# The opening of a scan kernel rearranged: x before the weights, weight products among the statistics, the second step's x and the first stores of silu asked for earlier

## The chip, the cores and the metric

The kernel runs on one core of a Trainium2 chip. The core has a matrix engine (TensorE, PE in the profile; its weight loads are listed apart, as PEld), a vector engine (VectorE, DVE), a scalar engine that applies functions and copies (ScalarE, ACT), a general engine (GpSimd, POOL) and an engine that here only issues transfers (SyncE, SP). Each engine works through its own instructions in the order in which they are written down; semaphores make one wait for another. Transfers between the chip's memory (DRAM) and the core run on 16 DMA engines, whoever issues them. Matrix products land in PSUM, which has eight banks.

The metric is the device time of one execution in microseconds (us), as a median of several.

## The reference

The input x is 4 images of 128 channels by 96 by 96 pixels, all in 32-bit floats. It is normalised in groups of four channels, goes through the block below, and is added to the result. Cut to what matters:

```python
def _scan1d(x, ...):                       # x: sequences of 9216 steps, 128 channels
    t = _grouped1x1(x, in_proj_w, in_proj_b, G)            # 128 -> 512, in 4 groups
    u, gate = (t[:, :HID], t[:, HID:])                     # HID = 256
    u = jax.nn.silu(u)
    u = depthwise_conv(u, dw_w)                            # 5 taps along the sequence
    s = _conv1x1(u, ssm_in_w)                              # 256 -> 32
    a = DMIN + (DMAX - DMIN) * jax.nn.sigmoid(_conv1x1(u, ssm_delta_w, ssm_delta_b))
    bb = jnp.tanh(_conv1x1(u, ssm_b_w, ssm_b_b))
    cc = jnp.tanh(_conv1x1(u, ssm_c_w, ssm_c_b))
    hst = recurrence(a, bb * s)                            # h[n] = a[n] * h[n-1] + bb[n] * s[n]
    u = u + _conv1x1(cc * hst + ssm_d[None, :, None] * s, ssm_out_w)
    u = _grouped1x1(u * jax.nn.sigmoid(gate), mix_w, mix_b, G)
    return _conv1x1(u, out_proj_w, out_proj_b)

seq_h = rows of the image one after the other;  seq_v = columns one after the other
y1, y2, y3, y4 = _scan1d(seq_h), _scan1d(seq_h reversed), _scan1d(seq_v), _scan1d(seq_v reversed)
x + fuse_w @ concat(y1, y2, y3, y4 put back in place) + fuse_b
```

The reference writes the recurrence with cumulative sums of logarithms. Three linear maps follow one another at the end (mix, output projection, fuse), so they can be multiplied into one matrix per direction beforehand.

## The kernel before

**Steps and units.** Two directions of the same image (forward and reversed) run together as s = 0 and s = 1. An image is scanned by columns, then by rows, in six steps each; a step has four positions p, and a unit is one step, position and direction, with 384 sequence elements in 128 by 384 tiles. Two units (s = 0, 1) make a pair; `pair(t)` on line 793 does the work of pair t, of which there are 192, and lets the later stages of a unit run six pairs (`LAG`) behind the first ones. The whole order is written out by hand (`tc.manual_schedule`): each engine gets its instructions in the order of the Python code.

**Stages of a pair.** `front` applies the input projection and silu to a quarter g of the following step (`in_proj`, line 486, products on PE from `x_in`; `silu`, line 493, on ScalarE into the tile `sil`, half of the channels for j = 0 and half for j = 1). `conv` and `conv_less` (613, 622) are the depthwise convolution of the j = 0 channels as products on PE. The j = 1 channels get it by `taps` (639): the first tap on ScalarE (line 649), the other four on VectorE (line 651), one after the other through the two PSUM banks TAPS, so that a pair's first tap cannot start before the last tap of the pair before. `proj` (663) takes u to the four small maps on PE; its evacuations (lines 683 to 689, tiles `tm` and `t`) are on ScalarE. `scan` (707) is the recurrence on VectorE. From pair 6 on come the gates, the output map, and `accumulate` (738), which applies the folded matrix `w_fin` and adds into `acc`.

**Transfers of x.** `x_in[s]` holds the step's x. `after_front` (460) asks for the next step's x as soon as a quarter's products have read the old one: rows of j = 1 for the quarter g, and after the last quarter the rows of j = 0 for all four quarters. The input projection of a quarter needs the j = 0 rows of all quarters and the j = 1 rows of its own. `keep_silu` (473) stores finished quarters of `sil` to DRAM, 770 KB each, because the second half of the steps reads the first half's silu again, mirrored. `load_chunks` (405) and `stats_chunks` (410) load the next image in chunks `xs` and take its statistics with `bn_stats` on VectorE. All these transfers are issued by SP, one after the other; the issue of a transfer waits until its target is free.

**The opening.** Before the first input projection the kernel needs the mean and variance of the first image. `load_x` (278) loads x in eight transfers into `acc`, and VectorE takes `bn_stats` of 24 chunks of 384 columns (line 282). In between, `load` (273) asks on ScalarE's queue for the three weight arrays: `small` (biases and taps), `fuse` (output, fuse and mix matrices) and `main` (input projection and small maps). PE multiplies the final matrices together as soon as `fuse` is there: eight products into `w_of` (line 364, evacuated on line 367), eight into `w_fin` (lines 371, 374), and twelve products with a single column for the bias `b_fin` (line 379). `stay_busy` (284) adds products whose result nobody reads. `stats_finish` (176) is a generator: it yields after each part, so that its caller puts other work between. Its parts: the aggregate of the statistics (line 184), a product with `gmean` that averages over the group (187), the same for the variance (199), the square root on ScalarE (207), the load of the silu table (209), the scaling of the input weights into `wn` (226), and products for the biases `bnorm` (235 and line 134). Then `start` (1001) runs the first step's projections in bursts and its silus, and the first pair's taps.

A 32-bit product shows as two matmul rows in the profile, one for each of its passes through the array. Line 134 is a helper, `mm`, through which most products go; tile names tell them apart.

Of the kernel before, what the change touches and what calls it, by code (L numbers as in the profile page):

```python
# [47 lines left out]
P = 128  # L48
# [8 lines left out]
R = 4  # L57
# [10 lines left out]
def conv_preact_kernel(  # L68
# [9 lines left out]
    nc = tc.nc  # L78
# [96 lines left out]

    def stats_finish(b):

# [94 lines left out]

    def load(src, name, pool=wp):
        t = pool.tile(list(src.shape), F32, tag=name, name=name)
        nc.scalar.dma_start(t, src)
        return t

    def load_x(chunks):
        for c, n in chunks:
            nc.sync.dma_start(accf[:, bass.ds(c * SC, n * SC)], xr[b0, :, bass.ds(c * SC, n * SC)])  # L280
            for e in range(c, c + n):
                nc.vector.bn_stats(stats_of(b0)[:, e, :], accf[:, bass.ts(e, SC)])

    def stay_busy(n):
        if n:
            nc.tensor.matmul(  # L286
                bank(free[0] ^ 1)[:, :n], w_fin[:, 0, 0, :],
                w_fin.rearrange("p d j c -> p (d j c)")[:, :n], start=True, stop=True,
                skip_group_check=True,
            )  # L290

# [32 lines left out]
    nc.vector.tensor_scalar_mul(  # L324
        w_proj[:, :, 2 * MH : 3 * MH], w_proj[:, :, 2 * MH : 3 * MH], 0.5
    )


# [17 lines left out]
    for s in range(2):  # L346
        for p in range(R):
            for k in range(2):
# [9 lines left out]
                )  # L358

    w_of = pp.tile([P, 4, 2, P], F32, name="w_of")  # L360
    for d in range(4):
        for j in range(2):
            pt = bank(2 * (d % 4) + j)
            nc.tensor.matmul(  # L364
                pt[:, :P], w_out[:, bass.ts(j, P)], w_fuse[:, d, :], start=True, stop=True
            )
            nc.scalar.copy(w_of[:, d, j, :], pt[:, :P])
    for d in range(4):
        for j in range(2):
            pt = bank(2 * (d % 4) + j)  # L370
            nc.tensor.matmul(
                pt[:, :P], w_mix[:, j, :], w_of[:, d, j, :], start=True, stop=True
            )
            nc.scalar.mul(w_fin[:, d, j, :], pt[:, :P], 0.5)
    pb = bank(0)
    terms = [(w_of[:, d, j, :], b_mix[:, j : j + 1]) for d in range(4) for j in range(2)]
    terms += [(w_fuse[:, d, :], b_out) for d in range(4)]
    for i, (lhsT, rhs) in enumerate(terms):
        nc.tensor.matmul(
            pb[:, 0:1], lhsT, rhs, start=(i == 0), stop=(i == len(terms) - 1)  # L380
        )
    nc.scalar.activation(b_fin, pb[:, 0:1], AF.Identity, bias=b_fuse)
    for _ in range(4):
        stay_busy(512)
    prep.__exit__(None, None, None)
# [45 lines left out]

    def front_parts(i, banks):
# [12 lines left out]
        if fresh(step):  # L445
            yield from compute_front(step, g, banks)
# [54 lines left out]

    def compute_front(step, g, banks):
# [160 lines left out]
    def proj(i, banks, apart=False):  # L663
# [129 lines left out]
    def pair(t):  # L793
# [104 lines left out]
        if t >= NU // 2 - 4:  # L898
            load_last(t)

        keep_silu((1, 2, 1, 0)[t] if t < R else 0)

# [131 lines left out]
    with tc.manual_schedule(  # L1034
        engines={
            nc.tensor.engine, nc.vector.engine, nc.scalar.engine, nc.gpsimd.engine, nc.sync.engine
        }
    ):
        start()
        for t in range(NU // 2):  # L1040
            pair(t)
        tail()
# [79 lines left out]
```

## Time and profile before

| | us |
|---|---|
| median of 4 runs | 1839.06 (1837.08 to 1843.52) |
| the profiled execution, time | 1835.29 |
| the profiled execution, span | 1833.5 |
| PE busy | 1806.9 (99% of the span) |
| ScalarE, VectorE, GpSimd busy | 1566.9, 1450.4, 1424.4 |

The profile is of one execution. Its page gives the busy time of each engine. The "windows" view gives the same for stretches of the span, with the clock that TensorE was granted (1.00 is full speed), the busy share of the DMA engines and the rate at which they moved data. The "chain of waits" is followed back from the last instruction: at each step to what released it. The "timeline" lists instructions in order of time, with like ones merged. Times in these views are in us from the span's start.

### The profile page before, as it was taken

The numbers are of one execution on the slowest core, as the hardware profiler recorded it, in microseconds if no ns is written. First come the engines' busy times: TensorE is split into PE (matmuls) and PEld (weight loads), VectorE is DVE, ScalarE is ACT, GpSimd is POOL, SyncE is SP. The second block draws the span as 40 slices with busy tenths as digits, with TensorE's granted clock in tenths as the row PEclk, the third lists the DMA queues.
The fourth block names the chain that finished last, engine by engine and source line by source line (L and its number), as shares of the span: only waits on it lengthen the run. The fifth ranks groups of instructions, "written<-read, shape, count | busy, mean of one in ns | idle before, by whom it ended". The sixth has DMA issues, their size and how long they took to land.

```text
span 1833.5 us, 57282 instructions
## 1 busy us (share of the span) xinstructions
PE 1806.9 (99%) x24068; PEld 653.9 (36%) x24068; DVE 1450.4 (79%) x1451; ACT 1566.9 (85%) x2762; POOL 1424.4 (78%) x1469
## 2 busy tenths in 40 slices
PE   7999999999999999999999999999999999999998
PEld 4233333333333333333333333333333333333333
DVE  5788878877878888877778888877877778777886
ACT  5888888988888888888898888888888888888974
POOL 2487887778777888787877888787877788887785
PEclk9999999999999999999999999999999999999999
DMA  6755563444975566244696547443576634635434
GB/s 206 186 193 180 159 191 113 161 143 142 301 233 181 168 182 199 101 143 140 209 299 208 165 162 211 136 154 110 162 233 226 231 127 152 192 105 178 148 122 156
DMA packets 147825, 321.18 MB, mean 175 GB/s; under 512 B 14192, under 2 KB 115696, under 8 KB 147568
## 3 DMA queue, kind: packets, MB, share of 16 engines
q1 hardware_dynamic: 147136, 316.56, 54.1%
q8 instruction: 190, 3.11, 0.7%
q10 hardware_dynamic: 432, 0.96, 0.1%
q14 instruction: 67, 0.55, 0.1%
HBM read 185.21 MB, written 132.25 MB: 173 GB/s over the span
## 4 chain that ended last, share of the span: by engine, by line
PE 95%; ACT 2%; DMA 1%; DVE 1%; issue 0%; SPq 0%; POOL 0%; ACTq 0%; DVEq 0%; POOLq 0%
PE psum L134 81%; PE psum L520 8%; PE psum L514 5%; DMA x_in<-in_xs 1%; ACT sil L495 0%; PE psum L286 0%; DMA fuse<-in_fuse 0%; DVE u L600 0%; ACT t L701 0%; PE psum L364 0%; ACT psum L649 0%; ACT t L689 0%; DMA out<-acc 0%; ACT u L632 0%; DVE psum L651 0%
## 5 line engine op out<-in xcount | busy, mean ns | idle before, releaser
L651 DVE SCALAR_TENSOR_TENSOR psum<-sil,small,psum 128x768 f32<-128x768 f32 x576 | 588.9, 1022 | 34.2 <-ACT psum L649 8.5
L134 PE MATMUL psum<-u,w_fin 128*32 128x384 f32 x6176 | 552.4, 487 | 0.2 <-ACT t L689 0.2
L600 DVE SCALAR_TENSOR_TENSOR u<-gate,psum 128x768 f32<-128x768 f32 x376 | 349.7, 952 | 253.9 <-ACT gate L537 117.7
L134 PE MATMUL psum<-u,main 128*32 128x384 f32 x6144 | 536.3, 490 | 0.1
L770 POOL TENSOR_TENSOR acc<-ys,acc 128x384 f32<-128x384 f32 x374 | 410.8, 1119 | 34.0 <-ACT ys L751 10.0
L724 POOL TENSOR_TENSOR t<-t,t 64x384 f32<-64x384 f32 x191 | 236.3, 1237 | 156.7 <-PE psum L514 79.3
L134 PEld LDWEIGHTS psum<-u,w_fin 128*32 128x32 f32 x6176 | 189.1, 110 | 321.5 <-issue 220.9
L134 PEld LDWEIGHTS psum<-u,main 128*32 128x32 f32 x6144 | 181.6, 110 | 327.9 <-issue 201.5
L691 POOL TENSOR_SCALAR t<-tm 64x384 f32<-64x384 f32 x191 | 177.1, 927 | 153.2 <-ACT tm L683 105.0
L528 ACT COPY psum<-u 128x768 f32<-128x768 f32 x352 | 276.7, 799 | 21.6 <-DVE u L651 10.2
L134 PE MATMUL psum<-sil,band 128*32 128x384 f32 x3072 | 286.1, 488 | 3.1 <-ACT ys L753 3.1
L725 POOL TENSOR_TENSOR t<-t,t 64x384 f32<-64x384 f32 x191 | 246.7, 1292 | 15.0
L520 PE MATMUL psum<-t,main 32*128 32x384 f32 x1536 | 242.1, 515 | 3.3 <-ACT psum L528 2.6
L649 ACT ACTIVATE psum<-sil,small 128x768 f32<-128x768 f32 x192 | 174.1, 907 | 63.9 <-DVE u L600 54.1
L537 ACT ACTIVATE gate<-psum,bnorm 128x384 f32<-128x384 f32 x384 | 192.8, 582 | 28.8 <-PE psum L514 26.8
L692 POOL TENSOR_TENSOR t<-t,tm 64x384 f32<-64x384 f32 x192 | 195.1, 1016 | 15.3
L651 DVE SCALAR_TENSOR_TENSOR u<-sil,small,psum 128x768 f32<-128x768 f32 x192 | 194.9, 1015 | 7.8
L495 ACT ACTIVATE sil<-psum,bnorm 128x385 f32<-128x385 f32 x384 | 192.1, 584 | 4.6 <-PE psum L134 2.4
L134 PE MATMUL psum<-sil,less 64*32 64x384 f32 x3072 | 168.2, 495 | 0.0
L514 PE MATMUL psum<-x_in,wn 32*128 32x384 f32 x768 | 162.0, 528 | 2.4 <-ACT u L632 1.3
L753 ACT COPY ys<-psum 128x384 f32<-128x384 f32 x281 | 130.1, 477 | 30.1 <-PE psum L134 27.1
L134 PEld LDWEIGHTS psum<-sil,band 128*32 128x32 f32 x3072 | 89.8, 109 | 174.7 <-issue 93.3
(92 smaller groups left out, 1503.0 us busy)
## 6 DMA issues: line engine op xcount, KB each, us to landing
sil<-sil SPq DMA_DIRECT2D x128, 770.0 KB, 6.9
kept<-gate SPq DMA_DIRECT2D x80, 768.0 KB, 3.8
gate<-kept SPq DMA_DIRECT2D x76, 768.0 KB, 5.2
x_in<-in_xs SPq DMA_DIRECT2D x192, 96.2 KB, 2.5
out<-acc SPq DMA_DIRECT2D x48, 384.0 KB, 8.2
acc<-in_xr SPq DMA_DIRECT2D x38, 384.0 KB, 7.2
xs<-in_xr SPq DMA_DIRECT2D x72, 192.0 KB, 4.9
x_in<-in_xs SPq DMA_DIRECT2D x184, 48.1 KB, 4.0
```

The costliest lines, as they stand in the source:

```text
L134: nc.tensor.matmul(o[r, : rhs.shape[-1]], lhsT, rhs, start=start, stop=stop, skip_group_check=True)
L495: nc.scalar.activation(sils[step][:, s, j, g, :], bank(bk)[:, : N + 1], AF.Silu, bias=bn[:, 1:2] if j else bn[:, 4 + g : 5 + g],)
L514: nc.tensor.matmul(bank(to)[:, :N], stats[un["b"]][0][r, s, :], x_in[s][r, q, off : off + N], start=True, stop=True)
L520: nc.tensor.matmul(bank(SSM + 2 * s + j)[:, :N], w_so[r, bass.ts(j, P)], z[r, :], start=bi not in seeded, stop=True, skip_group_check=True)
L528: nc.scalar.copy(psum[:, SSM + 2 * s : SSM + 2 * s + 2, :N], us[bi][:, s])
L537: nc.scalar.activation(gv[:, s, j, :], bank(to[2 * s + j])[:, :N], AF.Tanh, bias=bn[:, 2 + j : 3 + j], scale=0.5,)
L600: nc.vector.scalar_tensor_tensor(v, g, 1.0, pz, ALU.add, ALU.mult)
L651: nc.vector.scalar_tensor_tensor(us[i][:, :, 1, :] if k == K - 1 else part, src, w_tap[:, k : k + 1], part, ALU.mult, ALU.add,)
L692: nc.gpsimd.tensor_mul(ta[0:64, p, :], tb[0:64, :], tm[0:64, :])
L724: engine.tensor_mul(ta[0:64, p, :], tb[64:P, :], ta[64:P, p, :])
L725: engine.tensor_add(tb[0:64, :], ta[0:64, p, :], tb[0:64, :])
L770: adder.tensor_add(part, y, part)
```

## The change

It touches the opening and the first two pairs; from there on each engine's instructions come in the same order as before. What it does:

- **Loads.** `fuse` and `main` are asked for on SP's queue: `fuse` after 22 of the 24 chunks of x, `main` after the last. `small` stays where it was.
- **Scalings** of `b_proj` and of a part of `w_proj` go from VectorE to GpSimd, behind the building of the convolution bands.
- **Weight products.** PE first does three products of 512 columns from a piece of x (chunks 10 and 11) into bank 7, whose result nobody reads. Then come the eight products into `w_of`, with one evacuation of 256 columns for two of them. The products into `w_fin` are now in `fold(d)`, two products and one evacuation each: `fold(0)` after the aggregate, `fold(1)` and `fold(2)` after the mean, `fold(3)` after the square root; then the twelve single-column products, ahead of line 235's product. `stay_busy` is gone. `b_fin` is added up on VectorE.
- **First step.** In `start` the second step's x is asked for in six transfers: the j = 0 rows after the first four bursts, the j = 1 rows after the fifth and after the eighth. The four stores of the first step's silu are issued together at the end of `start`, instead of one, two and one in the first three pairs.
- **First pair.** The first tap of the second pair is issued in the middle of the silus of the second step's first quarter (two ahead of it, two behind), instead of ahead of them.

```diff
@@ load, load_x @@
-    def load(src, name, pool=wp):
+    def load(src, name, pool=wp, queue=nc.scalar):
         t = pool.tile(list(src.shape), F32, tag=name, name=name)
-        nc.scalar.dma_start(t, src)
+        queue.dma_start(t, src)
         return t
...
     load_x([(0, 1), (1, 2), (3, 3)])
     w_small = load(small, "small")
-    load_x([(6, 4)])
-    w_out_fuse = load(fuse, "fuse", pp)
-    load_x([(10, 4)])
-    w_main = load(main, "main")
-    load_x([(14, 4), (18, 4), (22, 2)])
+    load_x([(6, 4), (10, 4), (14, 4), (18, 4)])
+    w_out_fuse = load(fuse, "fuse", pp, nc.sync)
+    load_x([(22, 2)])
+    w_main = load(main, "main", wp, nc.sync)
...
@@ stats_finish(b, after_std=None) @@
             nc.scalar.activation(std, var, AF.Sqrt)
-
+            after_std()
             nc.scalar.activation(first_table, std[:, 0:1], AF.Silu)
...
@@ the weight products @@
-    nc.vector.tensor_scalar_mul(b_proj[64:P, 0:1], b_proj[64:P, 0:1], 0.5)
-    nc.vector.tensor_scalar_mul(
+    nc.gpsimd.tensor_scalar_mul(b_proj[64:P, 0:1], b_proj[64:P, 0:1], 0.5)
+    nc.gpsimd.tensor_scalar_mul(
         w_proj[:, :, 2 * MH : 3 * MH], w_proj[:, :, 2 * MH : 3 * MH], 0.5
     )
...
+    def fold(d):
+        pt = bank((4, 5, 0, 1)[d])[:, : 2 * P]
+        for j in range(2):
+            nc.tensor.matmul(
+                pt[:, bass.ts(j, P)], w_mix[:, j, :], w_of[:, d, j, :], start=True, stop=True
+            )
+        nc.scalar.mul(w_fin[:, d].rearrange("p j c -> p (j c)"), pt, 0.5)
+
+    with tc.manual_schedule(engines=engines):
+        for _ in range(3):
+            nc.tensor.matmul(
+                bank(7), accf[:, bass.ds(10 * SC, P)], accf[:, bass.ds(10 * SC, 512)],
+                start=True, stop=True,
+            )
+        for d in range(4):
+            pt = bank(d)[:, : 2 * P]
+            for j in range(2):
+                nc.tensor.matmul(
+                    pt[:, bass.ts(j, P)], w_out[:, bass.ts(j, P)], w_fuse[:, d, :],
+                    start=True, stop=True,
+                )
+            nc.scalar.copy(w_of[:, d].rearrange("p j c -> p (j c)"), pt)
+        pieces = stats_finish(b0, lambda: fold(3))
+        next(pieces)
+        fold(0)
+        next(pieces)
+        fold(1)
+        fold(2)
+        next(pieces)
+        pf = bank(7)
...
+        for i, (lhsT, rhs) in enumerate(terms):
+            nc.tensor.matmul(
+                pf[:, 0:1], lhsT, rhs, start=(i == 0), stop=(i == len(terms) - 1)
+            )
+        for _ in pieces:
+            pass
+        nc.vector.tensor_add(b_fin, pf[:, 0:1], b_fuse)
...
@@ compute_front(step, g, banks, half=False) @@
         for s, j in parts:
             silu(step, g, s, j, banks[2 * s + j])
+            if half and (s, j) == (0, 1):
+                yield
...
@@ proj @@
             if i == 0 and (e, j) == (0, 1):
-                front(R, (5, 4, 2, 3))
+                first = front_parts(R, (5, 4, 2, 3), half=True)
+                next(first)
+                next(first)
+                first_tap(2)
+                for _ in first:
+                    pass
...
@@ pair @@
-        if not back:
+        if not back and t:
             first_tap(i + 2)
-            if t:
-                front(t + R, FRONT if banks == PROJ else (5, 4, 2, 3))
+            front(t + R, FRONT if banks == PROJ else (5, 4, 2, 3))
...
-        keep_silu((1, 2, 1, 0)[t] if t < R else 0)
...
@@ start @@
-        pieces = stats_finish(b0)
-        for wait in (0, 256, 512, 0, 0):
-            next(pieces, None)
-            stay_busy(wait)
...
+        def load_rows(j, r):
+            for s in range(2):
+                load_front(1, s, slice(64 * s + 32 * j, 64 * s + 32 * j + 32), r)
+
         for g in range(R):
             burst(0, g)
+        load_rows(0, slice(0, R))
         for g in range(R):
             silus(0, g)
         new_u(0)
         for g in range(R):
             burst(1, g)
+            if g in (0, R - 1):
+                load_rows(1, slice(min(g, 1), g + 1))
             silus(1, g)
-            after_front(0, g)
+            to_keep.append((0, g))
             if g < 2:
                 taps(0, (g,))
             if g == 1:
                 conv(0, head_banks(0))
                 conv_less(0, head_banks(0))
         taps(0, (2, 3, 4))
+        keep_silu(R)
```

More of the change, by code (lines that the diff above doesn't have):

```diff
@@ L174, in stats_of, with stats_finish @@
         return stats[b]
-    def stats_finish(b):
+    def stats_finish(b, after_std=None):
         mv = sp.tile([P, 2], F32, tag="mv", name=f"mv_{b}")
@@ L282, in load_x @@
                 nc.vector.bn_stats(stats_of(b0)[:, e, :], accf[:, bass.ts(e, SC)])
[L284 to L290, printed above, removed]
     b0 = phases[0][0]
@@ L321, in conv_preact_kernel @@
     w_so = w_main[:, bass.ts(2, HID)]
-    nc.vector.tensor_scalar_mul(b_proj[64:P, 0:1], b_proj[64:P, 0:1], 0.5)
-    nc.vector.tensor_scalar_mul(
-        w_proj[:, :, 2 * MH : 3 * MH], w_proj[:, :, 2 * MH : 3 * MH], 0.5
-    )
     def less_of(p):
@@ L358, in conv_preact_kernel @@
                 )
+    nc.gpsimd.tensor_scalar_mul(b_proj[64:P, 0:1], b_proj[64:P, 0:1], 0.5)
+    nc.gpsimd.tensor_scalar_mul(
+        w_proj[:, :, 2 * MH : 3 * MH], w_proj[:, :, 2 * MH : 3 * MH], 0.5
+    )
+    engines = {
+        nc.tensor.engine, nc.vector.engine, nc.scalar.engine, nc.gpsimd.engine, nc.sync.engine
+    }
     w_of = pp.tile([P, 4, 2, P], F32, name="w_of")
-    for d in range(4):
+    def fold(d):
+        pt = bank((4, 5, 0, 1)[d])[:, : 2 * P]
         for j in range(2):
-            pt = bank(2 * (d % 4) + j)
@@ L364, in conv_preact_kernel @@
             nc.tensor.matmul(
-                pt[:, :P], w_out[:, bass.ts(j, P)], w_fuse[:, d, :], start=True, stop=True
+                pt[:, bass.ts(j, P)], w_mix[:, j, :], w_of[:, d, j, :], start=True, stop=True
             )
[L367 to L370, printed above, removed]
+        nc.scalar.mul(w_fin[:, d].rearrange("p j c -> p (j c)"), pt, 0.5)
+    with tc.manual_schedule(engines=engines):
+        for _ in range(3):
@@ L371, in conv_preact_kernel @@
             nc.tensor.matmul(
-                pt[:, :P], w_mix[:, j, :], w_of[:, d, j, :], start=True, stop=True
-            )
[L374 to L381, printed above, removed]
@@ L382, in conv_preact_kernel @@
-    nc.scalar.activation(b_fin, pb[:, 0:1], AF.Identity, bias=b_fuse)
-    for _ in range(4):
-        stay_busy(512)
+                bank(7), accf[:, bass.ds(10 * SC, P)], accf[:, bass.ds(10 * SC, 512)],
+                start=True, stop=True,
+            )
+        for d in range(4):
[6 more added lines that the diff above has]
+            nc.scalar.copy(w_of[:, d].rearrange("p j c -> p (j c)"), pt)
@@ new lines, in conv_preact_kernel @@
+        pieces = stats_finish(b0, lambda: fold(3))
[6 more added lines that the diff above has]
+        pf = bank(7)
+        terms = [(w_of[:, d, j, :], b_mix[:, j : j + 1]) for d in range(4) for j in range(2)]
+        terms += [(w_fuse[:, d, :], b_out) for d in range(4)]
+        for i, (lhsT, rhs) in enumerate(terms):
+            nc.tensor.matmul(
+                pf[:, 0:1], lhsT, rhs, start=(i == 0), stop=(i == len(terms) - 1)
+            )
@@ L430, in front, with front_parts @@
             pass
-    def front_parts(i, banks):
+    def front_parts(i, banks, half=False):
         step, g = divmod(i, R)
@@ L445, in front_parts @@
         if fresh(step):
-            yield from compute_front(step, g, banks)
+            yield from compute_front(step, g, banks, half)
         if st == 0:
@@ L500, in silu, with compute_front @@
         )
-    def compute_front(step, g, banks):
+    def compute_front(step, g, banks, half=False):
         parts = [(s, j) for s in range(2) for j in range(2)]
@@ L1032, in start @@
         taps(0, (2, 3, 4))
[L1034 to L1038, printed above, removed]
+        keep_silu(R)
+    with tc.manual_schedule(engines=engines):
         start()
```

## The prediction

> **What bounds the kernel now.** I read the page first, then short windows, then the chain of waits, then single instructions of the first 85 us. The page says that TensorE (PE) is busy for nearly the whole span:
>
> ```profile
> PE 1806.9 (99%) x24068; PEld 653.9 (36%) x24068; DVE 1450.4 (79%) x1451; ACT 1566.9 (85%) x2762; POOL 1424.4 (78%) x1469
> ```
>
> So 27 us are left in which PE does nothing, and the change touches only the beginning, where they lie. After about 85 us PE never stops (35.00 of 35.00 us in 85 to 120), so what is saved or lost before that point arrives at the end in full. Of the windows of 2 us, these (columns: stretch and sum, busy time of PE, weight loads, VectorE, ScalarE, GpSimd, granted clock, DMA share, GB/s):
>
> ```profile
> 2.00:4.00 2.00, 0.00 (x0) 0.00 (x0) 0.21 (x2) 0.74 (x2) 1.81 (x9) 1.00 0.98 284
> 4.00:6.00 2.00, 0.00 (x0) 0.00 (x0) 0.50 (x1) 0.00 (x0) 1.93 (x7) 1.00 1.02 407
> ...
> 14.00:16.00 2.00, 2.00 (x13) 1.63 (x14) 2.00 (x5) 0.26 (x1) 0.00 (x0) 0.82 1.00 406
> 16.00:18.00 2.00, 2.00 (x4) 0.83 (x3) 2.00 (x5) 0.00 (x0) 0.00 (x0) 0.50 1.08 248
> ...
> 34.00:36.00 2.00, 0.00 (x0) 0.00 (x0) 1.86 (x3) 0.09 (x1) 0.00 (x0) 1.00 0.69 182
> ...
> 60.00:62.00 2.00, 0.88 (x16) 0.21 (x16) 1.97 (x2) 1.45 (x3) 0.00 (x0) 1.00 1.23 252
> 62.00:64.00 2.00, 1.29 (x20) 0.27 (x24) 1.93 (x3) 0.53 (x3) 0.00 (x0) 0.76 1.00 225
> 64.00:66.00 2.00, 2.00 (x16) 0.67 (x20) 1.93 (x3) 1.03 (x2) 0.00 (x0) 0.50 1.07 292
> ```
>
> Three places show. Up to 24 us the DMA engines are full (share 1.0) and PE waits for the statistics. At 34 and at 59 PE stands still, and after the second stop its clock is at half until 66.5 us. The chain of waits names both stops:
>
> ```profile
> 33.08 3.40 DMA x_in<-in_xs
> 36.48 0.14 issue
> ...
> 55.70 6.96 DMA x_in<-in_xs
> 62.66 0.04 issue
> ```
>
> Both are transfers of the next step's x, asked for last, at 33.08 and 55.70. From the timeline of the opening (start, length, engine, line, work):
>
> ```profile
> 10.57 8.44 DVE L282 BATCH_NORM_STATS2 bn<-acc 128x6 f32<-128x384 f32 x18
> 12.49 1.87 PEld L379 LDWEIGHTS psum<-small,w_of 128*128 128x128 f32 x16
> ...
> 14.30 1.03 PE L379 MATMUL psum<-small,fuse 128*128 128x1 f32 x8
> ...
> 15.20 5.38 PE L286 MATMUL psum<-w_fin 128*128 128x512 f32 x8
> ...
> 20.41 0.28 PE L187 MATMUL psum<-mv,gmean 128*128 128x1 f32 x2
> ...
> 23.07 0.39 PE L235 MATMUL psum<-gm,wn 128*128 128x4 f32 x2
> ```
>
> Here the last bn_stats ends at 19.01, the aggregate (0.80) at 19.84, L187 starts 0.57 later behind the filler L286, and L235, after which the input projections run, at 23.07. The first silu is at 24.61.
>
> **The change, part by part** (times of the old timeline, against the profiled execution).
>
> *x ahead of the weights.* Summing GB/s over the windows, the engines had moved 0.6 MB at 4 us, 1.4 at 6, 2.3 at 8, 3.1 at 10, 4.0 at 12, 4.8 at 14, 5.6 at 16. Old order: all 5.68 MB (x 4.72, fuse 0.52, main 0.39, small 0.04) pass by 16.2 and the last x, issued at 6.0 with 11.5 to landing, lands at 17.5: 1.3 later. New order: last x is byte 5.29 MB, so 15.3 + 1.3 = 16.6; fuse byte 4.90, 14.3 + 1.2 = 15.5. The last two bn_stats (0.47 pitch, 0.56) then end at 17.6, the aggregate at 18.45. L187 can start at 18.5 instead of 20.41: **-1.9**. VectorE is rid of L323 (0.15) and L324 (0.64); it waits for transfers now, so they are inside that figure. On GpSimd, done with its bands at 11 and next at work at 40, the two lie free; behind them waits nothing before 40. Two issues (0.39, 0.45) move from ScalarE's queue to SP's; SP had issued all of x by 6.4 and the engines are full until 22, so first step's x, issued behind them, still passes at the same byte.
>
> *Filler and weight products.* The fillers need chunk 10 (2.8 MB, lands about 10.5); six passes at 0.86 (L286 before 18.7) or 0.43 (after) end at 14.3 to 15.6, and leave the clock full. Fuse at 15.5: 16 passes of L372 (old L364). At full clock L371 shows 7 passes in 0.83, 0.12 each: 1.9, and the first fold's 4 passes 0.5, done at 17.9, ahead of the 18.5. ScalarE's 16 evacuations of 0.27 become 8 of twice the width; between 0.27 and the 0.48 of a 128x384 copy, I take 0.37; they follow PE and hold nobody. L187 to L199 was 1.05; two folds (8 passes, 0.96) now stand between, 0.15 more. Then the loss: behind L199 (0.47) stand fold 3 (4 x 0.12 = 0.5) and the 24 single-column passes of the bias (L379: 12.60 to 15.33, 0.115 each, 2.75), and L235 waits behind them on PE. 18.5 + 1.2 + 0.47 + 0.5 + 2.75 = 23.4, against 23.07: **+0.3**. Without these passes it would be 18.5 + 2.66 = 21.2. The b_fin add on VectorE finds its operand ready.
>
> The clock adds to that. The means 0.82, 0.50 and 0.83 of the windows from 14 to 20 put it at half from 15.3 to 18.7, right after a stretch in which PE was "busy" with those single-column passes; they now stand straight before the input projections. The projections at half clock feed ScalarE (0.48 a silu) just as fast, so only the first comes later, by 0 to 0.5; I take **+0.2**. The opening sum is **+0.5**; bounds below. [...]
>
> *Step 1's x.* Rows for j=0 are asked for after the first bursts (about 26) instead of 32.7 to 33.08, in 6 transfers instead of 10. With 3.4 to landing they are there by 30, and the stop at 33.8 to 36.6 goes. What is late next: the second half of the projection of u (old 38.06) needs VectorE's last tap, 36.36, so it starts at 36.5. Then the next projection needs the taps of unit 2, whose L649 waits for that same tap (36.46) and ends with u at 41.59: 41.7 instead of 42.53. **-0.8**, not 2.8. The new order puts two silus ahead of this L649 and two behind it. The first two are done by 36.4 (PE serves them from 33.8, ScalarE needs 1.0) and free the banks of the next convolution; behind the waiting L649 stand the other two, tm and t, of which PE needs nothing before 40. From there ScalarE and PE, both full (16.04 and 16.44 of 16.5 us), carry it unchanged.
>
> *Stores of silu and step 2's x.* Four stores of 0.79 MB are issued at 34 instead of at 38.7, 44.4, 45, 50.8. One alone moved at about 0.35 MB/us (359 GB/s in 40 to 42): done at 45 to 46. The queue is then free, so step 2's j=0 rows, asked for at 54.2 and 54.9 (old 55.04 and 55.70, less 0.8), need about 3.4 (as at 33.08) and land at 57.6 to 58.3; PE wants them at 58.2 (old 59.03, less 0.8). The projection of unit 8 then starts at 59.2 instead of 63.92, and the next one follows after PE's own rows (2.8, 1.4, 0.9, 1.0) at 65.2, old 70.91; VectorE (u at 58.4, scan 1.8, four taps 4.15) is done at 64.4. So 5.7 in all by then, of which 0.8 was counted: **-4.9** (two stops of 1.5 and 1.3, and some 2 from the half clock). I give back **0.2** for a small rest of the wait. Behind the stores on SP stand step 2's first rows (wanted at 58) and the xs loads (L408), and in the new order the issues of xs wait until the first two stores have landed. VectorE comes to xs at 47 and can wait until 48.1 (two bn_stats 1.0, four taps 4.15, before PE's 53.3); 0.6 MB at 0.2 MB/us after 45 is 48. Tight: priced at nothing here, and as rival 4 if late.
>
> Sum: +0.5 - 0.8 - 4.9 + 0.2 = **-5.0**: 1835.29 to 1830.3 on the profiled execution, which lies 3.8 under the median; on the median 1839.06 it is **1834.0**.
>
> **The rivals.**
> 1. *The opening gains.* If the bias passes hide, L235 is at 21.2, -1.9 in place of +0.5: -7.4, **1831.7**. For it: the products are short. Against: 24 x 0.115 is measured, and L235 is behind them in order.
> 2. *The products run at half clock.* A pass is then 0.236 (L364: 16 in 3.78). 20 passes from 15.5 end at 20.2, L187 1.7 late, the folds 0.9 more: about -2.4, **1836.7**. [...]
> 3. *Step 2's x is still late,* by one of the two stops and the half clock (3): -2, **1837**. For it: 1540-byte rows run at 215 to 248 GB/s (x_in, 16 to 22 us).
> 4. *The stores take the place of the wait (slower).* If they run at the 0.19 to 0.2 MB/us that 50 to 54 shows (181, 191 GB/s, share full), 3.15 MB end at 52 and xs lands at 55, not 48. VectorE's bn_stats (1.0) and the four taps behind it end at 60.2; u of unit 6 goes from 53.3 to 60.3, all later waits are covered, 65.2 becomes 72.2 against 70.91: +1.3, with the opening's 0.5 **1840.9**. It passes the old time when xs lands after about 53.2. Against it: at 50 to 54 loads were mixed in, four stores alone are not. [...]
>
> **How the numbers follow.** Forecast 0.52, rivals 0.15, 0.13, 0.12, 0.08. Bounds of the opening, -1.9 to +3.1 (rivals 1 and 2); of the first stop, 0 to -2.8; of the second, -2 to -5.2. Range **1830.5 to 1840.0**: from a little below rival 1 over rivals 2 and 3 to the edge of rival 4, the runs themselves being 1837.08 to 1843.52; the forecast's own is 1832 to 1836. A measurement tells about 0.3% (5.5 us) from no change. The forecast is just short of that: 45% of it lies beyond, with rival 1 that is **0.38** faster; slower by 0.3% needs more than rival 4's price, **0.05**; the rest, **0.57**, within.
>
> **What would show it.** Right: L187 near 18.5, L235 near 23.4, a half clock near 23 to 27, no x_in wait over 0.5 in the first 70 us, PE full from 37 to 70 but for 1 us. Wrong: a DMA wait on bn_stats of xs near 47, or an idle PE with a half clock at 60. The forecast falls if xs or step 2's x lands late, or the opening differs from +0.5 by more than 2.

## The result, and the profile after

The changed kernel is slower, by little: 1840.11 us (median of 54 runs, 1835.64 to 1846.92) against 1836.31 for the kernel before in the same comparisons (78 runs, 1831.23 to 1846.47). The ratio is **1.0015 [1.0008, 1.0022]**, some 2.8 us; the means of the runs lie 2.8 apart, their medians 3.8. The forecast was 1834.0 and a gain of 5.0; the measured time lies just above its range, on the other side of no change. (The forecast was put on the 1839.06 of four runs; over all runs before is 2.8 lower, which would have made it 1831.3.)

The profiled execution took 1841.47 us, span 1839.7. That is 1.4 above its median, and before's 1835.29 is 1.0 below its own, so of the 6.2 between the two profiles 2.4 belong to these two executions. How long the clock is at half differs from run to run, and the time with it: of the 80 runs of before beside the experiments below, the 26 with a mean granted clock of 0.996 or more took 1831.2 to 1836.5 us, the 35 with 0.993 or less 1839.5 to 1846.2, and the profile of before has 0.996. The page of the changed kernel:

```profile
PE 1806.1 (98%) x24062; PEld 652.7 (35%) x24062; DVE 1449.4 (79%) x1450; ACT 1566.6 (85%) x2753; POOL 1425.3 (77%) x1471
```

PE's work is the same (1806.9 before), so what grew is time in which it does nothing: 33.6 us instead of 26.6. The windows of the changed kernel show where (stretch and sum, PE, weight loads, VectorE, ScalarE, GpSimd, granted clock, DMA share, GB/s):

```profile
4.00:6.00 2.00, 0.00 (x0) 0.00 (x0) 1.10 (x3) 0.00 (x0) 1.93 (x7) 1.00 0.91 294
6.00:8.00 2.00, 0.00 (x0) 0.00 (x0) 0.00 (x0) 0.00 (x0) 1.70 (x5) 1.00 0.94 309
...
28.00:30.00 2.00, 2.00 (x37) 1.62 (x30) 0.24 (x4) 1.88 (x4) 0.00 (x0) 0.50 0.00 0
...
34.00:36.00 2.00, 2.00 (x20) 0.42 (x20) 0.40 (x2) 1.43 (x3) 0.00 (x0) 0.50 0.49 130
...
60.00:62.00 2.00, 0.00 (x0) 0.00 (x0) 1.93 (x3) 0.00 (x0) 0.00 (x0) 1.00 0.57 158
62.00:64.00 2.00, 1.13 (x8) 0.46 (x12) 1.96 (x4) 1.24 (x2) 0.00 (x0) 0.50 0.84 228
64.00:66.00 2.00, 2.00 (x16) 0.69 (x12) 1.86 (x3) 1.58 (x4) 0.00 (x0) 0.50 1.07 315
```

Three things are new. From 4 to 8 us the loads run at 294 and 309 GB/s, where before had 407 in 4 to 6. The projections run at half clock: the half clock starts at 27.9 and lasts 10.2 us, where before had it for 3.4 us from 15.3 and full clock from there to 63. And the stop of PE at 34 is gone, but one at 60 is still there, with a longer half clock behind it. The chain of waits names the links:

```profile
5.73 13.90 DMA acc<-in_xr
19.66 1.03 DVE bn L282 x2
...
21.66 0.35 PE psum L187 x2
...
23.91 2.57 PE psum L388 x24
...
49.55 8.05 DMA xs<-in_xr
...
62.87 8.73 PE psum L134 x96
```

The opening hangs on the last piece of x (landed at 19.63) and on the 24 single-column passes (L388). The stop at 60 is no longer the step's x but `xs`, the next image's chunk. The waits from 24 to 85 us say the same (engine, line, what it waited for: us in total, times, longest):

```profile
PE psum L134 <- DVE u L662: 5.1, 3, 3.0
...
DVE bn L421 <- DMA xs<-in_xr: 4.3, 1, 4.3
```

No wait for `x_in` is left among them. The same view of the kernel before:

```profile
PE psum L134 <- DMA x_in<-in_xs: 5.6, 3, 2.8
...
PEld psum L134 <- DMA x_in<-in_xs: 2.4, 2, 2.0
```

Beside the chain, ScalarE's timeline from 30 us shows what the half clock does (start, length, work, idle before and its cause):

```profile
30.11 1.05 ACT L504 ACTIVATE sil<-psum,bnorm 128x385 f32<-128x385 f32 x2 [0.23 <-PE psum L134]
31.39 2.01 ACT L504 ACTIVATE sil<-psum,bnorm 128x385 f32<-128x385 f32 x4 [0.23 <-PE psum L134]
...
37.42 0.80 ACT L645 COPY u<-psum 128x768 f32<-128x768 f32 x1 [1.99 <-PE psum L134]
```

ScalarE, which feeds VectorE's taps, waits for PE here: 0.23 ahead of two groups of silus, then 1.99 for the convolution that line 645 copies into u. Before had ten silus on end without a gap:

```profile
24.61 4.84 ACT L495 ACTIVATE sil<-psum,bnorm 128x385 f32<-128x385 f32 x10 [0.59 <-PE psum L134]
```

From the timelines of the two profiled executions, stage by stage (u is the end of a pair's last tap, VectorE's line 651 before and 662 after; u0 the first pair's):

| stretch | before | after | difference | forecast |
|---|---|---|---|---|
| start to line 187 | 20.41 | 21.66 | +1.25 | -1.9 |
| line 187 to 199 | 1.05 | 1.19 | +0.1 | +0.15 |
| line 199 to 235 | 1.61 | 3.49 | +1.9 | +2.1 |
| line 235 to the first silu | 1.54 | 1.52 | 0 | +0.2 |
| first silu to u0 | 11.76 | 15.01 | +3.25 | 0 |
| u0 to u2 (step 1's x) | 11.39 | 10.44 | -0.95 | -0.8 |
| u2 to u3 (`xs`) | 5.61 | 9.41 | +3.8 | 0 |
| u3 to u6 (step 2's x) | 22.65 | 20.03 | -2.6 | -4.7 |
| u6 to the end | 1757.5 | 1757.0 | -0.5 | 0 |

The last row shows that what is won or lost by u6 does arrive at the end. Rows two to four, step 1's x and the end agree with the forecast within some 0.5; the start, the half clock and the `xs` wait do not, and step 2's x brought little over half of what was put on it.

### The profile page after: what moved, and what is told of

Same layout as the page of the kernel before. It is cut to its first block, busy times and chain, and to the rows that moved or that the text cites. A ratio compares the mean times of both kernels' runs of the same rounds, so it can differ in the third digit from the quotient of the medians.

```text
span 1839.7 us, 57260 instructions
## 1 busy us (share of the span) xinstructions
PE 1806.1 (98%) x24062; PEld 652.7 (35%) x24062; DVE 1449.4 (79%) x1450; ACT 1566.6 (85%) x2753; POOL 1425.3 (77%) x1471
## 4 chain that ended last, share of the span: by engine, by line
PE 95%; ACT 2%; DMA 1%; DVE 1%; SPq 0%; issue 0%; POOL 0%; DVEq 0%; ACTq 0%; POOLq 0%
PE psum L134 81%; PE psum L531 8%; PE psum L525 5%; DMA acc<-in_xr 1%; DVE psum L662 0%; DMA xs<-in_xr 0%; ACT sil L504 0%; DVE u L611 0%; SPq L280 0%; ACT t L717 0%; ACT psum L660 0%; ACT t L705 0%; DMA out<-acc 0%; DVE u L662 0%; ACT u L643 0%
## 5 line engine op out<-in xcount | busy, mean ns | idle before, releaser
L539 ACT COPY psum<-u 128x768 f32<-128x768 f32 x352 | 276.8, 799 | 20.6 <-DVE u L662 10.2
```

Source lines behind the costliest of these rows:

```text
L539: nc.scalar.copy(psum[:, SSM + 2 * s : SSM + 2 * s + 2, :N], us[bi][:, s])
```

## The experiments

Each kernel was timed beside the kernel before, in three groups, each on one chip; ratios are to that group's runs of before (medians 1836.51, 1840.0 and 1838.33). In ratio, 0.1% is 1.8 us. My theory after the result was: the new opening loses several us in place of 0.5, the stores lose through `xs`, and step 1's x alone is good. The rival: the opening is neutral, and everything lost is lost by the stores.

**1. The parts one by one.** `e_x` is the kernel before with only the earlier x of step 1 and the tap amid the silus:

```diff
         for g in range(R):
             burst(0, g)
+        load_rows(0, slice(0, R))
...
             burst(1, g)
+            if g in (0, R - 1):
+                load_rows(1, slice(min(g, 1), g + 1))
             silus(1, g)
-            after_front(0, g)
+            to_keep.append((0, g))
...
-                front(R, (5, 4, 2, 3))
+                first = front_parts(R, (5, 4, 2, 3), half=True)
+                next(first)
+                next(first)
+                first_tap(2)
+                for _ in first:
+                    pass
```

> The old opening and the old times of the silu stores; only the second step's x is asked for earlier and the first pair's tap stands among the silus. If the earlier request is a gain by itself (it takes the wait of 2.8 us near 34 us away, of which the taps on VectorE let 0.8 through), the kernel is 0.8 to 1 us faster than before, with the stop near 60 us still there, and the clock at full until then. If the request brings nothing because the taps set the pace anyway, it is the same as before within 0.3 us.

Measured: **0.9974 [0.9961, 0.9987]**, 1831.37 us. The gain is larger than either value expected, and the clock was not full until 60 us: it was at half for 13.7 us from 20.3.

`e_x_st` adds the early stores to it:

```diff
         taps(0, (2, 3, 4))
+        keep_silu(R)
...
-        keep_silu((1, 2, 1, 0)[t] if t < R else 0)
```

> As the run before, with the four silu stores issued together at the end of the start. If the stores cause the loss (xs lands behind them, VectorE waits some 4 us for it at the third pair, PE stops for 3 us and its clock halves), this kernel has that stop although its opening is the old one, and is 1 to 3 us slower than the kernel without them. If the stores do what they were forecast to do (step 2's x in time, xs in time), it is 4 to 5 us faster than before.

Measured: **0.9994 [0.9982, 1.0006]**. Its chain of waits has the transfer that was rival 4:

```profile
43.70 8.12 DMA xs<-in_xr
```

VectorE waits 3.6 us for it here, and from u2 to u3 it is 8.75 us instead of 5.74 in `e_x`. The wait and the stop of PE came as expected, the half clock behind the stop did not (1.00 throughout from 21.3 to 70).

`e_open_x` is the whole change with the stores as they were before:

```diff
         taps(0, (2, 3, 4))
-        keep_silu(R)
...
+        keep_silu((1, 2, 1, 0)[t] if t < R else 0)
```

> The whole change but with the silu stores at their old times. If the opening is the main loss (first silu 3.2 us late, then the half clock that lasts until the first taps are done, 6.5 late there), this is 3 to 6 us slower than before and the trace shows the first silu near 28 and a half clock from 28. If the stores alone are the loss, it is 1 us faster than before or better.

Measured: **0.9997 [0.9983, 1.0010]**. The total is neither of the expected ones, though the trace has what the first of them described: the first silu at 29.8, with a half clock from 27.1. The table below says why: what step 1's x gains stands against it.

`e_loads_old` is the whole change with the weights asked for as before:

```diff
-    load_x([(6, 4), (10, 4), (14, 4), (18, 4)])
-    w_out_fuse = load(fuse, "fuse", pp, nc.sync)
-    load_x([(22, 2)])
-    w_main = load(main, "main", wp, nc.sync)
+    load_x([(6, 4)])
+    w_out_fuse = load(fuse, "fuse", pp)
+    load_x([(10, 4)])
+    w_main = load(main, "main")
+    load_x([(14, 4), (18, 4), (22, 2)])
```

> The whole change but with the three weight arrays asked for as before, on ScalarE's queue and between the pieces of x. If x behind one queue is what makes the last piece late (19.6 us instead of 17.5), the last bn_stats ends near 19 and L187 starts near 20 again, 1.5 to 2 us earlier than in the changed kernel, which shows in the total. If the last piece is late for another reason, it lands near 19.6 again and the time is that of the changed kernel.

Measured: **1.0006 [0.9994, 1.0017]**, 0.09% (1.7 us) under the changed kernel, which is within the uncertainty of 0.14%. The trace is plainer: the last piece of x landed at 17.52, the last bn_stats ended at 18.97 and L187 started at 19.96, 1.70 earlier than in the changed kernel, as expected if the order of the loads makes x late. Its `xs` landed 8.52 us after the request, with a wait of 4.6.

Four of these kernels form a square:

| | stores as before | four stores early | the stores cost |
|---|---|---|---|
| old opening | 0.9974 | 0.9994 | +0.20% (3.7 us) |
| new opening | 0.9997 | 1.0015 | +0.18% (3.3 us) |
| the new opening costs | +0.23% (4.2 us) | +0.21% (3.9 us) | |

The lower right corner is the changed kernel's own ratio. Each difference is uncertain by 0.14 to 0.19%, and both rows and both columns agree. The two costs are of one size, so the rival (a neutral opening) falls; step 1's x alone gains 4.8 us [2.4, 7.2].

**2. The stores: their volume, or their place ahead of `xs`?** If the queue is the cause, the stores are harmless once the two `xs` loads are asked for first, or once the four are spread. `e_x_st_xs` is `e_x_st` with that order:

```diff
         taps(0, (2, 3, 4))
+        load_chunks(2)
         keep_silu(R)
...
-        if t + 1 < NU // 2:
+        if t + 1 < NU // 2 and t != 1:
             load_chunks(t + 1)
```

> All four stores at the end of the start as in the change, with the old opening, but the two xs loads of the third pair asked for just ahead of them. If the stores do harm only through these loads, VectorE's wait (some 4 us) and PE's stop behind it are gone and the kernel is 3 to 5 us faster than the same kernel with xs behind the stores (1835.6), about 1831 or a little better. If four stores at once hold up more than that (the next xs, the second step's x), it stays above 1833.

Measured: **0.9954 [0.9936, 0.9973]**, 0.40% under `e_x_st` with the same transfers; across two groups this is uncertain by 0.22%, and the medians themselves (1831.2 and 1835.6) lie 0.24% apart. Of its waits from 24 to 85 us, these are all on transfers:

```profile
PEld psum L134 <- DMA x_in<-in_xs: 0.4, 1, 0.4
...
PE psum L134 <- DMA x_in<-in_xs: 0.3, 1, 0.3
```

No wait for `xs`, and hardly one for the second step's x, as the forecast had described; from u2 to u3 it is 5.75 us again, 3.0 less than in `e_x_st`.

`e_x_st2` keeps `xs` where it was and spreads the stores instead:

```diff
         taps(0, (2, 3, 4))
+        keep_silu(2)
...
-        keep_silu((1, 2, 1, 0)[t] if t < R else 0)
+        keep_silu((1, 1, 0, 0)[t] if t < R else 0)
```

> The old opening, the second step's x earlier, and the four silu stores spread so that two go at the end of the start, one in the first and one in the second pair, none in the third. If only the crowd of four ahead of xs does harm, two stores (1.6 MB, 4.4 us at 359 GB/s) are through before xs is asked for, the queue is empty when the second step's last rows are asked for (near 55), the stop near 60 goes too, and this is 1 to 2.5 us faster than the kernel with the stores at their old times (1831.4). If any store ahead of xs holds it up, VectorE waits for xs at the third pair again and the time is the same or worse.

Measured: **0.9952 [0.9937, 0.9967]**. The same source ran once more in the third group:

> The old opening, the second step's x earlier, two stores at the end of the start and one in each of the next two pairs, again, beside the repaired change on one chip. If its gain is real it is 0.4 to 0.5% under before here too; if part of it was the kernel before being slow on that chip, it comes to 0.25%.

Measured: **0.9971 [0.9958, 0.9983]**. Neither of the two profiles shows a wait for `xs`. So the four stores at once ahead of `xs` are the cause; but whether stores asked for early and well gain anything over `e_x` (0.9974) is not settled: the two ratios of the spread stores stand 0.22 and 0.03% under that, each from another group.

**3. The opening: the bias passes.** `e_open_noterms` is `e_open_x` without the twelve single-column products:

```diff
-        for i, (lhsT, rhs) in enumerate(terms):
-            nc.tensor.matmul(
-                pf[:, 0:1], lhsT, rhs, start=(i == 0), stop=(i == len(terms) - 1)
-            )
         for _ in pieces:
             pass
-        nc.vector.tensor_add(b_fin, pf[:, 0:1], b_fuse)
+        nc.vector.tensor_copy(b_fin, b_fuse)
```

> The changed opening with the old store times, with the twelve single-column products for the folded bias left out (the output's bias is then only that of the fuse step). If they are what stands between the variance and the scaled input weights, the product of line 235 follows the variance within 1.1 us instead of 3.3 and the kernel is 2.2 us faster than the same with them (1836.9); if they also are what halves the clock for the projections, the half clock at 27 to 37 is gone and it is 4 to 5 us faster. If other work takes their place on the path, it gains under 1 us.

Measured: **0.9981 [0.9966, 0.9995]**, 0.16% (2.9 us) under `e_open_x`; across two groups this is uncertain by 0.19%. The timeline is plainer. PE in `e_open_noterms`:

```profile
20.42 0.50 PE L199 MATMUL psum<-ex,gmean 128*128 128x1 f32 x4
20.78 0.69 PE L358 MATMUL psum<-w_of,fuse 128*128 128x128 f32 x4
21.93 0.38 PE L235 MATMUL psum<-gm,wn 128*128 128x4 f32 x2 [0.46 <-DVE wn L226]
```

From 199 to 235 are 1.51 us instead of the 3.57 of `e_open_x`: the passes are worth 2.06 there, as step 199 to 235 of the forecast had it (2.1). The clock was still at half for 10.2 us, from 23.5, so the single-column passes alone are not what throttles the projections.

**4. The opening: the load queue.** `e_open_2q` is `e_open_x` with three of the pieces of x asked for on ScalarE's queue:

```diff
+            queue = nc.scalar if c in (1, 6, 14) else nc.sync
-            nc.sync.dma_start(accf[:, bass.ds(c * SC, n * SC)], xr[b0, :, bass.ds(c * SC, n * SC)])
+            queue.dma_start(accf[:, bass.ds(c * SC, n * SC)], xr[b0, :, bass.ds(c * SC, n * SC)])
```

> The changed opening with the old store times, but three of the eight pieces of x (chunks 1, 6 to 9 and 14 to 17) asked for on ScalarE's queue; the weights stay behind x on SP's. If one queue alone is what lets the DMA engines move only 300 GB/s from 4 to 8 us, that stretch shows above 400 and the last piece of x lands near 17 instead of 19.6 to 20.5; the kernel is then 2 to 3 us faster than with one queue (1836.9). If the engines finish their shares at different times because transfers of other shapes follow behind, the last piece stays near 20 and the time is the same.

Measured: **0.9999 [0.9984, 1.0014]**, no change against `e_open_x`. The windows show that the rate did come back (430 and 406 GB/s against 357 and 382 in `e_open_x`):

```profile
4.00:6.00 2.00, 0.00 (x0) 0.00 (x0) 1.30 (x3) 0.00 (x0) 0.18 (x2) 1.00 1.08 430
6.00:8.00 2.00, 0.00 (x0) 0.00 (x0) 1.61 (x4) 0.00 (x0) 1.00 (x3) 1.00 0.98 406
```

The last piece landed at 16.4, and VectorE's statistics ended at 19.04. But in this execution the clock fell earlier, at 20.8, and for 20.5 us, right over the single-column passes:

```profile
23.30 3.41 PE L389 MATMUL psum<-small,w_of 128*128 128x1 f32 x16
...
26.58 1.84 PE L389 MATMUL psum<-small,fuse 128*128 128x1 f32 x8
```

5.25 us for 24 passes that take 2.87 at full clock. In this one profile the transfer was mended, and the clock took the gain. Of the 12 runs 8 have a mean granted clock of 0.993 or less, of `e_open_x`'s 12 one.

The unchanged total decides nothing on the queues, as the clock differed too, and why the rate rose between 4 and 8 us was not tested.

**5. The opening: the clock.** `e_open_fill` is `e_open_noterms` with two 512-column products that nobody reads, one after `fold(0)`, one after `fold(3)`, as dense work ahead of the projections:

```diff
+    def fill(k=512):
+        nc.tensor.matmul(
+            bank(7)[:, :k], accf[:, bass.ds(10 * SC, P)], accf[:, bass.ds(10 * SC, k)],
+            start=True, stop=True,
+        )
...
-        pieces = stats_finish(b0, lambda: fold(3))
+        def last_fold():
+            fold(3)
+            fill()
+        pieces = stats_finish(b0, last_fold)
         next(pieces)
         fold(0)
+        fill()
```

> The changed opening with old store times and, as in the run that left them out, without the twelve single-column products of the folded bias; added are two products of 512 columns whose result nobody reads, one behind the first fold and one behind the last, 1.7 us of dense work at full clock. If the clock is halved because too little dense work stands in the 3.4 us ahead of the projections (in the run without them some 1.4 of 3.4), the projections now run at full clock in the trace, first silu to last tap takes 11.8 us instead of 13.4 to 15.1, and the kernel is 1 to 2.5 us faster than without the two products, although they put off the first silu by up to 0.8. If the clock follows from something else, the half clock stays and it is 0 to 1 us slower.

Measured: **0.9970 [0.9959, 0.9982]**, 0.11% (2 us) under `e_open_noterms`, uncertain by 0.18% (its profiled execution, 1838.80, is 6.3 above its median of 1832.5: step 2's x came late there, as in before). What the fillers do stands in its timeline and windows:

```profile
22.20 0.50 PE L199 MATMUL psum<-ex,gmean 128*128 128x1 f32 x4
...
23.09 1.02 PE L364 MATMUL psum<-acc 128*128 128x512 f32 x2
23.95 0.28 PE L235 MATMUL psum<-gm,wn 128*128 128x4 f32 x2
...
25.39 4.83 ACT L511 ACTIVATE sil<-psum,bnorm 128x385 f32<-128x385 f32 x10 [0.19 <-PE psum L134]
```

```profile
24.00:26.00 2.00, 2.00 (x75) 1.69 (x81) 0.39 (x3) 1.80 (x4) 0.00 (x0) 1.00 0.31 85
26.00:28.00 2.00, 2.00 (x67) 1.21 (x48) 0.29 (x5) 2.00 (x5) 0.00 (x0) 1.00 0.00 0
```

L235 comes 0.24 later after L199 than without the filler, the clock stays at 1.00, the ten silus run on end in 4.83, and from the first silu to u0 it is 11.74 us instead of 14.98. The 3.4 us of the expectation is the length that the half clock had in before (15.3 to 18.7); that the clock goes by the work in such a stretch was the author's guess, and no run shows it. The runs bear out the one profile: all 12 have a mean granted clock of 0.996 or more, of the 12 without the fillers 7.

Over all profiles this stretch falls into two groups. At full clock (before, `e_x_st`, `e_x_st_xs`, both runs with the stores spread, `e_open_fill`, `e_rep` below) it is 11.74 to 11.76. With a half clock (after, `e_x`, and every kernel of the new opening without the fillers) it is 13.4 to 15.1. So a half clock over the projections costs 1.7 to 3.4 us. Five of five profiles of the new opening without the fillers had it, and one of six of the old: in `e_x` the old fillers happened to run at full clock, were done at 18.0, PE stood idle until 19.93, and the clock fell at 20.3 for 13.7 us.

**6. All mended.** `e_rep` is the change with the old load order, the bias products back right behind the products into `w_of`, four fillers behind them instead of three ahead, the two fillers of step 5, and the stores spread:

```diff
+        nc.vector.tensor_add(b_fin, pf[:, 0:1], b_fuse)
+        for _ in range(4):
+            fill()
         pieces = stats_finish(b0, last_fold)
...
-        keep_silu(R)
+        keep_silu(2)
...
+        keep_silu((1, 1, 0, 0)[t] if t < R else 0)
```

> The change repaired at the three places: the weights asked for as before, the bias products right behind the eight products into w_of and the dense products behind them and two more among the folds, the stores spread as two, one and one. The folds still stand among the statistics. If late x, the bias passes with the half clock behind them, and the crowd of stores are all that was wrong, it is as fast as the kernel with the old opening and the spread stores, 0.4 to 0.5% under before. If spreading the folds costs by itself, it is slower than that kernel by more than 1 us.

Measured: **0.9968 [0.9955, 0.9981]**, 1831.96 us: 0.32% under the kernel before, and 0.47% under the changed kernel. In its profile's chain of waits:

```profile
21.99 0.86 PE psum L365 x2
22.85 0.12 PE psum L235 x2
...
24.11 2.23 ACT sil L513 x5
```

The last filler (L365) starts at 21.99, line 235's product follows it, the first silu is at 24.11, u0 is at 35.85, the earliest of all profiles, against 24.61 and 36.37 before. Yet `e_x_st2b`, with the whole old opening, stands at 0.9971 in the same group. So even mended, the new opening gains nothing in time that these runs can tell; what the mended kernels gain must then lie behind the opening. Its clock is steadier: all 9 runs of `e_rep` have a mean granted clock of 0.997 or 0.998, those of `e_x_st2b` 0.993 to 0.998.

## Why the prediction was wrong

The total was wrong in sign: +2.8 us [1.5, 4.0] measured, -5.0 forecast. By the square, the three parts of the sum, which add up by construction, are: the opening +4.2 (forecast +0.5), step 1's x -4.8 (forecast -0.8), the stores and step 2's x +3.3 (forecast -4.9 and +0.2). A change of under 0.3% either way was the likeliest of the forecast's three outcomes (0.57) and is what came, but from parts that cancel and not from its sum.

**"L187 can start at 18.5: -1.9".** This term failed. The byte count had the last piece of x at 16.6, from the rate of the old order; in after it landed at 19.63, 13.9 us after its issue, in `e_open_x` at 20.5, in `e_open_fill` at 19.0 and in `e_open_noterms` at 17.2. L187 came 1.25 later than in before, not 1.9 earlier. In all profiles of the old order the last piece landed between 17.2 and 18.0, and the eighteen bn_stats in a row, which end near 19.0, hid that. Rows of the kernel before could not price the rate of another order; the forecast took it as fixed. With two queues the rate rose to before's and the piece came at 16.4, earlier than in any profile with one; that is a single profile, and why the landing varies by 3.3 us between executions of like code stays open.

**"Behind L199 stand fold 3 and the 24 single-column passes: 2.75 ... L235".** Right: 3.49 us from L199 to L235, forecast 3.72, and 1.51 without the passes. Rival 1 falls with it.

**"The projections at half clock feed ScalarE just as fast; I take +0.2".** This term failed, and by the most within the opening: 3.25 us in the profiles, from 11.76 to 15.01. A half clock did come with the projections, but later than the forecast's 23 to 27 (from 27.9) and for 10.2 us instead of 3.4, and the projections do not feed ScalarE as fast: it waits 0.23 ahead of two groups of silus and 1.99 for the convolution. Nor do the single-column passes account for it: `e_open_noterms`, without them, had it, and in `e_x`, with them in the old place, the clock stayed full until 20.3. Nor was it for want of work on PE that the clock stayed at half: in after PE shows 2.00 busy of 2.00 us in each window from 28 to 38, at 0.50. Two dense products ahead of the projections kept it full (1.00 from 24 to 40 in `e_open_fill`); what the clock goes by was not shown.

**"Step 1's x: -0.8, not 2.8".** The mechanism was right in the profile: the wait near 34 is gone, the taps set the pace, u0 to u2 is 0.95 shorter. The measured -4.8 of `e_x` is more than this. Part of the rest stands in its profile: with the stores unmoved, step 2's x landed 5.02 us after its request at 58.64 instead of 6.96 after 55.70, with waits of 0.9 and 1.3 instead of 5.6 and 2.4 and no half clock behind. Why it was shorter was not tested; where the chains of waits name it, the landing took 4.7 to 7.6 us with the stores unmoved (six profiles) and 4.1 to 4.3 with the stores early or spread (`e_x_st2`, `e_x_st_xs`, `e_rep`). Another part stands in the runs: 35 of the 80 runs of before have a mean granted clock of 0.993 or less, one of the 8 of `e_x`, and of the 101 runs of all the experiments but `e_open_2q`, which all have this request, 9. So it seems to spare the kernel some half clock that the profile of before, at 0.996, does not have; no profile shows where.

**"Tight: priced at nothing here, and as rival 4 if late."** This is the step that failed in the stores. The forecast took 359 GB/s from one store alone and put `xs` at 48. Over 40 to 56 in after, with x_in rows and `xs` between the stores, it is 162 to 320 GB/s; `xs` took 8.05 us and landed at 57.6 (8.12 and 8.52 in `e_x_st` and `e_loads_old`). VectorE's four taps stand behind that bn_stats, so PE stood still from 59.9 to 62.87 and ran at half clock for 6.8 us: the sign of being wrong that the forecast had named. The late opening is not what did it, although it put the stores of after off to 40.1: in `e_x_st`, with the old opening and the stores at 34.3, as forecast, `xs` was as late. That is rival 4's mechanism, which had 0.08, and `e_x_st_xs` shows it by removing it; that rival 4's price (1840.9) is so near the measured 1840.1 is luck, as it has neither the opening's 4.2 nor the 4.8 of step 1's x. The waits that the stores were moved for did go: no x_in wait over 0.5 in after, as forecast.

With the opening and the stores repaired, the forecast's -5.0 is about what is measured: `e_rep` -5.9 us [-8.3, -3.5]. That the two agree is in part luck, because the forecast gave the gain to the wrong part. In `e_x`, with the stores unmoved, the stretch from u3 to u6 is 19.07 us, 3.6 less than before, and in three more kernels with unmoved stores 19.0 to 19.5 (in `e_open_fill` it is 24.74); so most of the 4.7 that was put on the stores came without them. Two tight places, the landing of the last piece of x and that of `xs`, were priced at their favourable end.

## What to carry to other kernels

Before a bulk store is moved earlier on a queue, list the small loads that come behind it and who waits for them: asking for the 0.4 MB of `xs` ahead of the 3.1 MB of stores was worth 3.0 us of its stretch in the profiles and 0.2 to 0.4% of the time. When dense work is taken out of the stretch ahead of a phase that is paced by another engine, count on half clock for much of that phase (6.8 to 20.5 us here, in all five profiles of the new opening without fillers), and try some dense filler ahead of it: two products cost 0.24 us on the path here and kept the clock full. And a transfer that lands behind other work shows in the trace no more than that it was in time: before a change puts it on the path, allow for the spread of its landings.

## What the runs showed of the hardware that was not expected

- A half clock that meets the projections stays long: 6.8 us in `e_loads_old`, 10.2 in after, `e_open_x` and `e_open_noterms`, 13.7 in `e_x`, 20.5 in `e_open_2q`, while PE had work nearly all the time (2.00 of 2.00 us from 28 to 38 in after); the same projections entered at 1.00 stay there (1.00 from 24 to 40 in `e_open_fill`). These lengths, and the 3.4 of before, are multiples of 3.4 us.
- The windows give 1.00 also where no clock is on record yet. In after, whose first clock record is at 17.6 us, the 512-column passes from 12.26 on start 0.85 us apart, as at half clock; two such passes in `e_open_fill` at 1.00 take 1.02 together.
- Single-column passes of 32-bit products took 0.12 us each at full clock (2.87 for 24 in after) and 0.22 at half (5.25 in `e_open_2q`).
- Nearly the same loads asked for on one queue, but for the small first array, moved 294 to 383 GB/s between 4 and 8 us, and 406 to 432 when two queues shared them.
- The last piece of x, asked for between 5.3 and 6.2 us, landed between 16.4 and 20.5, over kernels that differ little up to there.
